# Fetching only the used rows in 19 of the last layer's 187 gathers

## The chip, the cores and the metric

The kernel runs on one core of a Trainium2 chip. The metric is the device time of one execution in microseconds. The profile's line numbers are those of the kernel's file before the change.

## The reference

Four graph layers run on one adjacency matrix of 2708 nodes with 128 features. Each layer's output is added to its input and the sum is normalised. The last layer, which the change touches, forms a message for every pair of nodes and sums the messages weighted by the adjacency:

```
s = node_feats @ msg_w[:, :D].T
d = node_feats @ msg_w[:, D:].T
messages = gelu(s[:, None, :] + d[None, :, :] + msg_b)
aggregated = einsum('ijd,ij->id', messages, adj)
h = gelu(concat([node_feats, aggregated]) @ upd_w.T + upd_b) + node_feats
out = (h - mean(h)) / sqrt(var(h) + 1e-5) * ln_w + ln_b
x = layernorm(x + out)
```

The adjacency is sparse (a node has a handful of neighbours), so only the messages of neighbours matter.

## The kernel before, in words

The first two layers multiply with the adjacency as a dense matrix on TensorE. While they run, VectorE finds each row's nonzero entries in descending order: `V` holds their values and `LIDX` their column numbers, for 22 blocks of 128 rows with up to `SLOTS` = 24 slots. Rows are sorted by their number of neighbours; `PERM` names the row that stands at each place, and `RANK` the place of each row. Block `b` needs no more than `CAPS[b]` slots, from 21 in the first block to 2 in the last, 187 in all. A row with fewer neighbours than its block's cap has the value zero in the remaining slots of `V`.

The third layer gathers one neighbour's row for every row (tile `ga`, line 918, 22 gathers), reads the rows in sorted order from DRAM into `OWN` (four loads by SyncE's queue), and forms the shares, the new features `X3` (line 1061) and the products `yd` for the last layer. `yd` is scattered to the DRAM table `TD` in the order of rows (line 1052, 22 scatters issued by GpSimd).

The last layer works by blocks in the order of `TURN`. For the block at position `k`:

- `gathers(k)` issues one indirect DMA on GpSimd (POOL) for each slot (line 1150): row `LIDX[p, b, s]` of `TD` goes to partition `p` of `G[:, s, :]`. The tile `G` comes from a pool of four buffers.
- `terms(k)` makes the row's own product on TensorE.
- `messages(k)` adds it to all gathered rows on VectorE (line 1179, tile `M`) and applies gelu on ScalarE (lines 1180 and 1181).
- `diagonals(k)` makes a diagonal matrix of each slot's values of `V` on ScalarE (line 1171, tile `W`), and `update(k)` multiplies the messages with them on TensorE, accumulating over the slots (line 1143). A zero in `V` so takes a slot's row out of the sum.
- `added` and `norms` finish the rows on VectorE, for sets of one to four blocks, and `stores` scatters them to the output (line 1250, GpSimd).

The loop is software-pipelined: in step `k` come the stores that are ready, the gathers of `k + 1`, its terms, then messages, diagonals and update.

`conditions()` checks, once, that the sparse path is valid: line 1102 marks the slots with a value above zero, line 1105 counts them for each block within its cap, and the count is compared with the row's degree. A violation raises the flag that has the general, dense path run afterwards. `X3B` (line 1097) is an addition of all normalised rows and a bias, which the norms use later.

The order on each engine is the order in which the program issues its instructions: `pinned` chains every instruction of an engine to the one before it. Waits between engines are put in by the tile framework, from the regions of tiles that instructions read and write. DMAs issued by GpSimd take eight semaphores in turn, so each waits for the one eight before it.

Of the kernel before, what the change touches and what calls it, by code (L numbers as in the profile page):

```python
# [24 lines left out]
F32 = mybir.dt.float32  # L25
# [6 lines left out]
ALU = mybir.AluOpType  # L32
AX = mybir.AxisListType
# [3 lines left out]
P = 128  # L37
# [9 lines left out]
SLOTS = 24  # L47
CAPS = (21, 13, 12, 11, 11, 10, 10, 9, 9, 9, 8, 8, 8, 7, 7, 6, 6, 6, 5, 5, 4, 2)


TABLE = (("kk", 32), ("lane", 128), ("part", 1), ("lt", 128), ("ident", 128))


def table():

    import numpy as np

    p = np.arange(P)[:, None]
    cols = {
        "kk": np.broadcast_to(np.arange(32), (P, 32)),  # L60
        "lane": np.broadcast_to(np.arange(P), (P, P)),
        "part": p,
        "lt": p < np.arange(P),
        "ident": p == np.arange(P),
    }
    return np.concatenate([cols[n].astype(np.float32) for n, _ in TABLE], axis=1)


@with_exitstack
def sparse_path(  # L70
# [27 lines left out]
    nc = tc.nc  # L98
    N, D = x.shape
    NB = -(-N // P)  # L100
# [10 lines left out]
    def rows(b):  # L111
        return min(P, N - b * P)
# [4 lines left out]
    const = ctx.enter_context(tc.tile_pool(name="s_const", bufs=1))  # L117
# [14 lines left out]
            X[:, k, :], x[k.start * P : k.stop * P, :].rearrange("(b p) d -> p b d", p=P)  # L132
        )
    nc.sync.dma_start(X[: rows(NF), NF, :], x[NF * P :, :])
    TAB = const.tile([P, sum(w for _, w in TABLE)], F32, name="TAB")
    nc.scalar.dma_start(TAB, consts)
    part, at = {}, 0
    for name, w in TABLE:
        part[name] = TAB[:, at : at + w]
        at += w  # L140
    ident = part["ident"]
# [21 lines left out]
    for h in range(HEADS):  # L163
        k = slice(h * HD, (h + 1) * HD)
# [34 lines left out]
    V = const.tile([P, NB, SLOTS], F32, name="V")  # L199
    nc.gpsimd.memset(V, 0.0)  # L200
    LIDX = const.tile([P, NB, SLOTS], U32, name="LIDX")
# [5 lines left out]
    V_, S_, T_, G_ = nc.vector, nc.scalar, nc.tensor, nc.gpsimd  # L207
    newest = {}

    def pinned(i):  # L210

        e = i.ins.engine
        if e in newest:
            tc.add_manual_dep(
                i.ins, newest[e].name,
                mybir.DependencyInfo(mybir.DependencyClass.NoSync, mybir.DependencyReason.DATA),
                reason="order",
            )
        newest[e] = i.ins
        return i  # L220
# [80 lines left out]
    f = lists.tile([P, NB], F32, name="f")  # L301
# [602 lines left out]
    TD = dram.tile([NP, D], F32, name="TD")  # L904
    late = ctx.enter_context(tc.tile_pool(name="late", bufs=1))
    OWN = late.tile([P, NB, W_], F32, name="OWN")
    X3 = late.tile([P, NB, D], F32, name="X3")
    with (
        tc.tile_pool(name="l2", bufs=1) as one,
        tc.tile_pool(name="l2b", bufs=2) as sb,  # L910
# [147 lines left out]
        def norm3(k):  # L1058
            zs, t = mid[k]
            for i, b in enumerate(sets[k]):  # L1060
                pinned(S_.activation(  # L1061
                    X3[:, b, :], XO[:, b, :], AF.Identity, bias=t[:, 0, i : i + 1],
                    scale=t[:, 3, i : i + 1],
# [21 lines left out]
    TURN = tuple(range(17)) + (19, 17, 20, 18, 21)  # L1085
    SETS = ((0, 4), (4, 8), (8, 12), (12, 16), (16, 19), (19, 21), (21, 22))
    with (
        tc.tile_pool(name="l3", bufs=1) as one,
        tc.tile_pool(name="l3_g", bufs=4) as gp,
        tc.tile_pool(name="l3_w", bufs=2) as wp,  # L1090
        tc.tile_pool(name="l3_o", bufs=3) as op,
        tc.tile_pool(name="l3_s", bufs=3) as sb,
# [3 lines left out]
        pinned(V_.tensor_tensor(W3[:, D : 2 * D], W3[:, :D], WD, ALU.add))  # L1096
        pinned(V_.tensor_tensor(X3B, X3, LN_B.unsqueeze(1).to_broadcast([P, NB, D]), ALU.add))

        def conditions():

            has = one.tile([P, NB, SLOTS], F32, name="has")
            pinned(V_.tensor_scalar(has, V, 0.0, None, ALU.is_gt))
            count = one.tile([P, NB], F32, name="count")
            for b in range(NB):
                pinned(V_.tensor_reduce(count[:, b : b + 1], has[:, b, : CAPS[b]], AX.X, ALU.add))
            pinned(V_.tensor_tensor(count, count, OWN[:, :, W_ - 1], ALU.not_equal))
            pinned(V_.tensor_reduce(FL[:, 4:5], count, AX.X, ALU.max))

            odd = one.tile([P, NB], F32, name="odd")
            pinned(V_.tensor_tensor(odd, CNT, HAVE, ALU.not_equal))  # L1110
            pinned(V_.tensor_reduce(FL[:, 2:3], odd, AX.X, ALU.max))
            same = one.tile([P, NB, SLOTS - 1], F32, name="same")
            pinned(V_.tensor_tensor(same, V[:, :, 1:], V[:, :, : SLOTS - 1], ALU.is_equal))
            pinned(V_.tensor_tensor(same, same, V[:, :, 1:], ALU.mult))
            pinned(V_.tensor_reduce(FL[:, 3:4], same, AX.XY, ALU.max))


            gap = one.tile([P, NB], F32, name="gap")
            pinned(V_.tensor_tensor(gap, V[:, :, 0], OWN[:, :, W_ - 2], ALU.max))
            pinned(V_.tensor_tensor(gap, gap, V[:, :, 1], ALU.subtract))  # L1120
            pinned(V_.tensor_scalar(gap, gap, 4e-7, None, ALU.is_lt))
            pinned(V_.scalar_tensor_tensor(gap, PERMF, float(N), gap, ALU.is_lt, ALU.mult))
            pinned(V_.tensor_reduce(FL[:, 5:6], gap, AX.X, ALU.max))
            lim = one.tile([P, 2], F32, name="lim")
            pinned(V_.tensor_reduce(lim[:, 0:1], OWN[:, :, 2 * D : W_ - 2], AX.XY, ALU.max))
            pinned(V_.tensor_reduce(lim[:, 1:2], OWN[:, :, 2 * D : W_ - 2], AX.XY, ALU.min))
            pinned(V_.tensor_scalar(lim[:, 1:2], lim[:, 1:2], -1.0, None, ALU.mult))
            pinned(V_.tensor_tensor(lim[:, 0:1], lim[:, 0:1], lim[:, 1:2], ALU.max))
            pinned(V_.tensor_scalar(FL[:, 7:8], lim[:, 0:1], 200.0, None, ALU.is_gt))
            worst = one.tile([P, 1], F32, name="worst")  # L1130
            pinned(V_.tensor_reduce(worst, FL, AX.X, ALU.max))
            t = ps.tile([P, P], F32, name="xT_ps")
            pinned(T_.transpose(t[:1, :], worst, ident))
            pinned(V_.tensor_reduce(worst[:1, :], t[:1, :], AX.X, ALU.max))
            pinned(V_.tensor_scalar(flag, worst[:1, :], 0.0, None, ALU.is_gt))

        place = {k: (i, k - lo) for i, (lo, hi) in enumerate(SETS) for k in range(lo, hi)}
        ys, sums, mids, Gs, Ms, Ws, ready = {}, {}, {}, {}, {}, {}, []
# [6 lines left out]
        def gathers(k):  # L1145
            b = TURN[k]
            n = CAPS[b]
            G = Gs[k] = gp.tile([P, CAPS[0], D], F32, name="G")
            for s in range(n):
                pinned(G_.indirect_dma_start(  # L1150
                    G[:, s, :], None, TD,
                    bass.IndirectOffsetOnAxis(ap=LIDX[:, b, s : s + 1], axis=0),
                ))

        def terms(k):

            t = ps.tile([P, P], F32, name="xT_ps")
            pinned(T_.transpose(t, X3[:, TURN[k], :], ident))
            xT = sb.tile([P, P], F32, name="xT")
# [14 lines left out]
        def messages(k):  # L1174
            n = CAPS[TURN[k]]
            G, m = Gs.pop(k), mids[k][0]
            M = Ms[k] = wp.tile([P, CAPS[0] + 1, D], F32, name="M")
            s_ = m[:, :D].unsqueeze(1).to_broadcast([P, n, D])
            pinned(V_.tensor_tensor(M[:, :n, :], G[:, :n, :], s_, ALU.add))  # L1179
            pinned(S_.activation(M[:, n, :], m[:, D : 2 * D], AF.Gelu))  # L1180
# [17 lines left out]
        def stats(dst, src):  # L1198
            st = small.tile([P, 6], F32, name="bn_s3")
            pinned(V_.bn_stats(st, src))  # L1200
            pinned(V_.bn_aggr(dst, st))

        def added(k):
            i, j = place[k]
            h = ys[i][:, j, :]
            pinned(V_.tensor_tensor(h, h, X3[:, TURN[k], :], ALU.add))
            stats(sums[i][:, j, :], h)
# [39 lines left out]
        def stores(k):  # L1247
            while ready and ready[0][0] <= k:
# [5 lines left out]
                tc.declare_no_dep(i.ins, group="OUT", reason="each row has a place of its own")  # L1254
                tc.add_to_no_dep_group("OUT", i.ins)

        gathers(0)
        conditions()
        terms(0)
        diagonals(0)  # L1260
        for k in range(NB):
            if k + 1 < NB:
                stores(k + 1)
                gathers(k + 1)
                terms(k + 1)
            messages(k)
            if k + 1 < NB:
                diagonals(k + 1)
            update(k)
            if k:  # L1270
                added(k - 1)
                i, j = place[k]
                if not j:
                    g = norms(i - 1)
                    for done in g:
                        if k == NB - 1 and done:
                            break
# [521 lines left out]
```

## Time and profile before

| what | us |
|---|---|
| median of 3 runs | 708.85 |
| lowest and highest of them | 706.58 and 709.79 |
| profiled execution | 709.3 |
| its span | 707.5 |
| POOL busy in the span | 378.5 |
| DVE busy | 393.0 |
| PE busy | 451.2 |
| ACT busy | 272.4 |

The span is what the profile covers of the execution; 1.8 us lie around it. A busy time is a sum over stages with different limits, so it doesn't say by itself what bounds the kernel; the chain of work that ended last and the groups of instructions, with what ended the idle time before each, are read for that.

### The profile page before, as it was taken

How to read it: one execution, taken by the hardware profiler on the slowest of the kernel's cores; microseconds unless marked ns; L12 is line 12 of the kernel's file. 1: busy time of each engine (PE TensorE's matmuls, PEld its weight loads, DVE VectorE, ACT ScalarE, POOL GpSimd, SP SyncE). 2: the span in 40 equal slices, each digit the busy share in tenths (PEclk: the TensorE clock that was granted, in tenths of full speed). 3: DMA queues.
4: the chain of work that ended last, by engine and by line, in shares of the span. 5: the costliest groups of instructions: out<-in, count | busy, mean ns of one | idle time of the engine just before them, and what ended most of it. 6: DMA issues, size and time to landing. Idle time of an engine off the chain costs nothing.

```text
span 707.5 us, 8193 instructions
## 1 busy us (share of the span) xinstructions
PE 451.2 (64%) x2565; PEld 301.7 (43%) x2565; DVE 393.0 (56%) x1138; ACT 272.4 (38%) x719; POOL 378.5 (53%) x449
## 2 busy tenths in 40 slices
PE   5889999996164999997511502066646546747461
PEld 5745445663152444464311501055536435545451
DVE  4767999999983856640208834111171251434466
ACT  3145655772330100174411574055335424444330
POOL 7002001221246776036577677777777777777761
PEclk9579999998556999999755555566776857788665
DMA  9968999996294999875254111222122122211210
GB/s 296 406 245 309 415 415 379 324 374 224 101 386 153 419 418 415 311 216 191 85 181 128 42 52 40 53 54 52 52 53 55 53 53 53 53 52 52 54 48 13
DMA packets 44400, 128.68 MB, mean 182 GB/s; under 512 B 7983, under 2 KB 19523, under 8 KB 38716
## 3 DMA queue, kind: packets, MB, share of 16 engines
q0 software_dynamic: 16832, 75.13, 30.2%
q1 hardware_dynamic: 21116, 49.66, 19.7%
q10 hardware_dynamic: 6400, 3.29, 1.7%
q8 instruction: 22, 0.36, 0.2%
q14 instruction: 30, 0.25, 0.1%
HBM read 119.29 MB, written 8.81 MB: 181 GB/s over the span
## 4 chain that ended last, share of the span: by engine, by line
DVE 27%; POOL 24%; PE 19%; issue 14%; DMA 9%; ACT 6%; SPq 0%; POOLq 0%; DVEq 0%; ACTq 0%
POOL G L1150 17%; PE acc L753 12%; DVE IX L580 9%; DVE cand L565 5%; DMA G<-TD,LIDX 4%; PE z L753 3%; POOL ga L918 2%; DMA TOP<-in_high 1%; POOL TS L693 1%; ACT squares L257 1%; PE w_ps L355 1%; ACT XD L267 1%; ACT X L1061 1%; DMA nat<-in_adjo,PERM 1%; POOL ln_r L262 1%
## 5 line engine op out<-in xcount | busy, mean ns | idle before, releaser
L1150 POOL DMA_INDIRECT G<-TD,LIDX x187 | 177.4, 948 | 58.7 <-issue 52.4
L1143 PE MATMUL aT_ps<-W,M 128*128 128x128 f32 x418 | 91.0, 394 | 112.5 <-ACT M L1180 105.1
L1143 PEld LDWEIGHTS aT_ps<-W,M 128*128 128x128 f32 x418 | 80.9, 292 | 126.4 <-ACT M L1180 114.0
L1179 DVE TENSOR_TENSOR M<-G,sd_ps 128x1152 f32<-128x1152 f32 (+11 forms) x22 | 28.3, 1287 | 159.0 <-DMA G<-TD,LIDX 142.8
L753 PE MATMUL acc<-ah,XD 128*128 128x512 f32 (+1 forms) x264 | 113.7, 568 | 1.0 <-ACT XD L626 1.0
L580 DVE FIND_INDEX8 IX<-V,nat 128x8 uint32<-128x2707 f32 x33 | 97.8, 2970 | 0.0
L830 ACT ACTIVATE sign<-ah 128x1536 bf16<-128x1536 f32 (+1 forms) x44 | 57.7, 1327 | 37.1 <-issue 26.8
L753 PE MATMUL acc<-ah,HS 128*128 128x512 f32 x132 | 63.3, 615 | 12.1 <-ACT HS L866 12.1
L753 PEld LDWEIGHTS acc<-ah,XD 128*128 128x128 f32 x264 | 47.9, 196 | 44.5 <-issue 41.4
L536 POOL DMA_INDIRECT nat<-in_adjo,PERM x22 | 21.5, 979 | 81.5 <-DVE IX L580 55.4
L1171 ACT ACTIVATE W<-TAB,V 128x128 f32<-128x128 f32 x187 | 56.8, 390 | 0.0
L558 DVE MAX8 V<-nat 128x8 f32<-128x2707 f32 x12 | 35.7, 2976 | 26.6 <-DMA nat<-in_adjo,PERM 26.6
L1180 ACT ACTIVATE M<-sd_ps 128x128 f32<-128x128 f32 x22 | 6.1, 278 | 113.2 <-DVE M L1179 113.2
L753 PEld LDWEIGHTS acc<-ah,HS 128*128 128x128 f32 x132 | 25.4, 196 | 44.7 <-issue 29.3
L866 ACT ACTIVATE HS<-HS,DS 128x128 f32<-128x128 f32 x22 | 8.4, 399 | 78.0 <-DMA HS<-TH,PERM 48.8
L565 DVE MAX8 cand<-nat 128x8 f32<-128x338 f32 (+3 forms) x88 | 34.3, 461 | 2.8 <-DMA nat<-in_adjo,PERM 2.8
L251 POOL TENSOR_SCALAR ln_a<-SUM 128x4 f32<-128x4 f32 (+1 forms) x12 | 2.9, 238 | 61.1 <-DVE XD L649 33.2
L1250 POOL DMA_INDIRECT out_x<-yo,PERM x22 | 22.1, 1003 | 18.5 <-DVE yo L1229 11.3
L861 POOL DMA_INDIRECT HS<-TH,PERM x22 | 21.0, 957 | 19.6 <-DMA TH<-H 10.1
L1052 POOL DMA_INDIRECT TD<-yd,PERM x22 | 24.2, 1102 | 9.6 <-ACT yd L1048 4.1
L753 PE MATMUL acc<-ah,H 128*128 128x512 f32 (+1 forms) x88 | 28.1, 462 | 0.0
L693 POOL DMA_INDIRECT TS<-XD,RANK x22 | 21.6, 982 | 11.3 <-issue 5.4
(281 smaller groups left out, 862.6 us busy)
## 6 DMA issues: line engine op xcount, KB each, us to landing
ah<-in_adjL SPq DMA_DIRECT2D x22, 768.0 KB, 13.5
ah<-in_adjR SPq DMA_DIRECT2D x44, 330.0 KB, 5.5
TOP<-in_high SPq DMA_DIRECT2D x5, 1354.0 KB, 13.0
ah<-in_adjL SPq DMA_DIRECT2D x22, 256.0 KB, 7.2
G<-TD,LIDX POOLq DMA_INDIRECT x187, 2.5
OWN<-TS SPq DMA_DIRECT2D x3, 798.0 KB, 8.5
TA<-XD ACTq DMA_DIRECT2D x5, 264.0 KB, 2.8
TH<-H ACTq DMA_DIRECT2D x5, 256.0 KB, 10.2
```

What stands on the lines that cost most here:

```text
L558: pinned(nc.vector.max(V[:, b, 0:8], t))
L565: pinned(nc.vector.max(c[:, 8 * k : 8 * k + 8], t[:, at]))
L580: pinned(nc.vector.max_index(IX[:, b, s], V[:, b, s], t))
L693: i = G_.indirect_dma_start(TS, bass.IndirectOffsetOnAxis(ap=RANK[:, b : b + 1], axis=0), XD[:, b, :], None,)
L753: pinned(T_.matmul(acc[i][:, :w], weights[:, n, :], a[:, i * BANK : i * BANK + w], start=n == 0, stop=n == NB - 1,))
L830: pinned(S_.activation(m[:, : hi - lo], a, AF.Sign))
L1052: i = G_.indirect_dma_start(TD, bass.IndirectOffsetOnAxis(ap=PERM[:, b : b + 1], axis=0), yd[:, i, :], None)
L1143: pinned(T_.matmul(t, a, b, start=n == 0, stop=n == len(parts) - 1))
L1150: pinned(G_.indirect_dma_start(G[:, s, :], None, TD, bass.IndirectOffsetOnAxis(ap=LIDX[:, b, s : s + 1], axis=0),))
L1171: pinned(S_.activation(W[:, s, :], ident, AF.Copy, scale=V[:, b, s : s + 1]))
L1179: pinned(V_.tensor_tensor(M[:, :n, :], G[:, :n, :], s_, ALU.add))
L1250: i = G_.indirect_dma_start(out, bass.IndirectOffsetOnAxis(ap=PERM[:, b : b + 1], axis=0), h, None, bounds_check=N - 1, oob_is_err=False,)
```

## The change

A table `LIMITS` names, for 19 pairs of block and slot, how many rows of the block are used; rows are sorted by their number of neighbours, so the used ones are the first. Each of those gathers then fetches only that many rows: 849 of 2432. The four buffers of `G` become four tiles named `spaces`, taken in turn, and the slots of the first three that are gathered in part at first use are set to zero before (line 1282 of the changed file), so that the rows not fetched hold finite numbers; later uses leave there what an earlier block had fetched. `V` is zero in these places.

The check counts only slots that the table calls used: `USES`, a 128 x 528 mask, comes with the table of constants, is loaded by SyncE's queue before the loads of `OWN`, and is multiplied into the marks. A row with more neighbours than the table allows thus raises the flag. The 22 counts become one over all 24 slots.

```diff
+LIMITS = {
+    0: {13: 122, 14: 65, 15: 41, 16: 23, 17: 14, 18: 10, 19: 9, 20: 8},
+    1: {12: 85}, 2: {11: 97}, 4: {10: 41}, 6: {9: 56}, 9: {8: 12}, 12: {7: 40}, 17: {5: 62},
+    19: {4: 48}, 20: {3: 68}, 21: {0: 26, 1: 22},
+}
+def used(b, s):
+    return LIMITS.get(b, {}).get(s, P) if s < CAPS[b] else 0
...
-    TAB = const.tile([P, sum(w for _, w in TABLE)], F32, name="TAB")
-    nc.scalar.dma_start(TAB, consts)
+    W_TAB = sum(w for n, w in TABLE if n != "uses")
+    TAB = const.tile([P, W_TAB], F32, name="TAB")
+    nc.scalar.dma_start(TAB, consts[:, :W_TAB])
...
     X3 = late.tile([P, NB, D], F32, name="X3")
+    USES = late.tile([P, NB, SLOTS], F32, name="USES")
+    nc.sync.dma_start(USES.rearrange("p b s -> p (b s)"), consts[:, W_TAB:])
...
-        tc.tile_pool(name="l3_g", bufs=4) as gp,
...
-            pinned(V_.tensor_scalar(has, V, 0.0, None, ALU.is_gt))
+            pinned(V_.scalar_tensor_tensor(has, V, 0.0, USES, ALU.is_gt, ALU.mult))
             count = one.tile([P, NB], F32, name="count")
-            for b in range(NB):
-                pinned(V_.tensor_reduce(count[:, b : b + 1], has[:, b, : CAPS[b]], AX.X, ALU.add))
+            pinned(V_.tensor_reduce(count, has, AX.X, ALU.add))
...
-            G = Gs[k] = gp.tile([P, CAPS[0], D], F32, name="G")
+            G = Gs[k] = spaces[k % 4]
             for s in range(n):
+                m = used(b, s)
                 pinned(G_.indirect_dma_start(
-                    G[:, s, :], None, TD,
-                    bass.IndirectOffsetOnAxis(ap=LIDX[:, b, s : s + 1], axis=0),
+                    G[:m, s, :], None, TD,
+                    bass.IndirectOffsetOnAxis(ap=LIDX[:m, b, s : s + 1], axis=0),
                 ))
...
+        spaces = [one.tile([P, CAPS[0], D], F32, name=f"G{k}") for k in range(4)]
+        for k in range(4):
+            n = CAPS[TURN[k]]
+            some = [s for s in range(n) if used(TURN[k], s) < P]
+            if some:
+                pinned(V_.memset(spaces[k][:, some[0] : n, :], 0.0))
         gathers(0)
```

More of the change, by code (lines that the diff above doesn't have):

```diff
@@ L48 @@
 CAPS = (21, 13, 12, 11, 11, 10, 10, 9, 9, 9, 8, 8, 8, 7, 7, 6, 6, 6, 5, 5, 4, 2)
-TABLE = (("kk", 32), ("lane", 128), ("part", 1), ("lt", 128), ("ident", 128))
+LIMITS = {
[3 rows of a table added]
+}
+def used(b, s):
+    return LIMITS.get(b, {}).get(s, P) if s < CAPS[b] else 0
+TABLE = (
+    ("kk", 32), ("lane", 128), ("part", 1), ("lt", 128), ("ident", 128),
+    ("uses", len(CAPS) * SLOTS),
+)
 def table():
@@ L64, in table @@
         "ident": p == np.arange(P),
+        "uses": p < np.array([[used(b, s) for s in range(SLOTS)] for b in range(len(CAPS))]).ravel(),
     }
@@ L134, in sparse_path @@
     nc.sync.dma_start(X[: rows(NF), NF, :], x[NF * P :, :])
-    TAB = const.tile([P, sum(w for _, w in TABLE)], F32, name="TAB")
-    nc.scalar.dma_start(TAB, consts)
+    W_TAB = sum(w for n, w in TABLE if n != "uses")
+    TAB = const.tile([P, W_TAB], F32, name="TAB")
+    nc.scalar.dma_start(TAB, consts[:, :W_TAB])
     part, at = {}, 0
-    for name, w in TABLE:
+    for name, w in TABLE[:-1]:
         part[name] = TAB[:, at : at + w]
```

## The prediction, made before the changed kernel ran

> **What bounds the kernel now.** I read the slices of the page first, then its chain and groups, then the timeline of POOL. From 429 to 684 us POOL is the engine that never rests, while PE, DVE and ACT stand near half. The chain and the costliest groups say why:
>
> ```profile
> POOL G L1150 17%; PE acc L753 12%; DVE IX L580 9%; DVE cand L565 5%; DMA G<-TD,LIDX 4%; PE z L753 3%; POOL ga L918 2%; DMA TOP<-in_high 1%; POOL TS L693 1%; ACT squares L257 1%; PE w_ps L355 1%; ACT XD L267 1%; ACT X L1061 1%; DMA nat<-in_adjo,PERM 1%; POOL ln_r L262 1%
> ...
> L1150 POOL DMA_INDIRECT G<-TD,LIDX x187 | 177.4, 948 | 58.7 <-issue 52.4
> ...
> L1179 DVE TENSOR_TENSOR M<-G,sd_ps 128x1152 f32<-128x1152 f32 (+11 forms) x22 | 28.3, 1287 | 159.0 <-DMA G<-TD,LIDX 142.8
> ```
>
> The gathers are the largest item of the chain. Each holds POOL for 948 ns, and the idle time before them is 52.4 us of "issue", 0.30 us each: nothing holds them back, and one leaves every 1.25 us. DVE waits 142.8 us for their data. A stretch in the middle of the stage agrees (us; then busy us of PE, PEld, DVE, ACT, POOL; clock; DMA share; GB/s):
>
> ```profile
> 480.00:520.00 40.00, 21.48 (x102) 17.95 (x100) 7.76 (x17) 15.09 (x45) 30.23 (x33) 0.76 0.21 52
> ```
>
> POOL with 30.2 busy us plus its issue gaps is full; the DMA engines are at 0.21. So bytes saved are worth nothing by themselves; what counts is the time that a partial gather holds POOL. All 187 gathers have 128 rows, so no row of the trace shows that. The nearest rows are the direct copies that POOL issues early on, of 128 rows (L171, L172, L174), 32 rows (L166) and one row cut into 16 pieces (L179):
>
> ```profile
> L166 POOL DMA_DIRECT2D AJI<-in_a x4 | 2.0, 508 | 1.0 <-DMA W<-in_w 1.0
> ...
> L179 POOL DMA_DIRECT2D BIAS<-in_msg_b x2 | 1.0, 505 | 0.4 <-issue 0.3
> ...
> L171 POOL DMA_DIRECT2D W<-in_msgT x1 | 0.6, 568 | 0.0
> ...
> L172 POOL DMA_DIRECT2D W<-in_updT x1 | 0.5, 539 | 0.0
> L174 POOL DMA_DIRECT2D UB<-in_updT x1 | 0.5, 534 | 0.0
> ```
>
> A direct copy costs about 0.54 us with 128 rows and 0.50 with 16 or 32 pieces. The gather's 0.944 (its median) is 0.40 more, for the work on indices; whether that 0.40 goes by rows is the question.
>
> **What the Trainium skill says.** (1) "Perfetto Trace Analysis", DMA Instruction — SWDGE (GPSIMD): the profile ends such an instruction when the last descriptor is written, not when data lands. The trace agrees: gathers last 0.94 us, the median landing is 2.5. (2) "DMA: Bandwidth & Descriptors", Anatomy of one DMA: generating descriptors is a small part, and "You can emit a lot of descriptors before the incremental cost shows up". The direct copies agree (0.04 us for 112 more); for gathers nothing shows it. (3) The same page, Why a DMA increments its semaphore by 16: a transfer runs on the largest k up to 16 that divides its row count; some direct copies are excepted. 97, 41 and 23 rows would go through one DMA engine, 122 and 62 through two. No run shows it yet. (4) "SBUF — State Buffer", Who interferes with whom: a DVE operation with two SBUF inputs blocks a GpSimd instruction that reads SBUF. The trace agrees:
>
> ```profile
> 370.03 0.95 DVE L967 TENSOR_TENSOR OWN<-OWN 128x768 f32<-128x768 f32 x1
> 370.46 1.34 POOL L918 DMA_INDIRECT ga<-TA,LIDX  x1 [0.30 <-issue]
> 372.10 0.94 POOL L918 DMA_INDIRECT ga<-TA,LIDX  x1 [0.30 <-issue]
> ...
> 422.83 3.09 DVE L1097 TENSOR_TENSOR X3B<-X,LN_B 128x2816 f32<-128x2816 f32 x1 [11.35 <-ACT X L1061]
> ...
> 423.52 3.23 POOL L1052 DMA_INDIRECT TD<-yd,PERM  x1 [0.30 <-DMA TD<-yd,PERM]
> 428.80 1.29 POOL L1150 DMA_INDIRECT G<-TD,LIDX  x1 [2.05 <-DVE odd L1110]
> ```
>
> Indirect transfers that start while such an operation runs end 0.82 us after it (370.98 and 371.80; 425.92 and 426.75).
>
> **The change, part by part.**
>
> *Which gathers count.* Near the end the chain leaves POOL: the last gather of position 18 (issued at 663.75) lands, DVE adds at 668.18, and from there PE, ACT and DVE carry the chain through the norms to 702. The gathers of positions 19 to 21 lie beside that. So the three partial ones among them (68, 26 and 22 rows) save nothing, and 16 count: 733 rows kept of 2048, 1315 saved.
>
> *POOL per row.* Index part 0.40 us/128 = 3.1 ns a row, descriptor part 0.04/112 = 0.4 ns: 3.5 ns, times 1315 = 4.6 us. Bounds: none of it by rows, 0; all of 0.944 by rows, 7.4 ns x 1315 = 9.7 us. Below nothing: see the first rival. I take 4.6: the index part is the one that a direct copy lacks, and its natural unit is the index.
>
> *Landing.* On the chain this matters only for position 18, whose last gather has 62 rows. A descriptor occupies its engine for about 0.21 x 1.25 us/8 = 33 ns (estimate, 128 rows over 16 engines). If two engines take 31 rows each, that is 23 more than 8, 0.8 us later; if all 16 take part, nothing. I take 0.4. Elsewhere a late landing is covered: POOL waits for the gather eight before, 8 x 1.25 = 10 us, and 97 rows on one engine take 3.2 us beyond the fixed part of 2.5. If descriptors took over 80 ns each, that cover would go and POOL would stall; up to 3 us for all, kept for the range. The four buffers leave three blocks of slack as before.
>
> *Start of the stage.* G's four spaces now lie in pool "l3", and the order of instructions shows that X3B has come to wait for all scatters of TD (SWDGE semaphores), where it waited for PE and ACT alone. The last scatter is then not blocked: 0.96 instead of 3.23 us, and the first gather starts 2.3 us earlier, at about 426.5. But X3B is released there too and blocks it until 426.5 + 3.09 + 0.82 = 430.4, where it now ends at 430.1. If the gather wins, the second one ends at that 430.4 instead of 431.35. So +0.3 or -0.9; the masking operation on V and USES has now two SBUF inputs, up to 0.4 more on one gather. I take 0, between -0.9 and +0.7.
>
> *DVE.* Three memsets (1024, 128 and 128 elements; those at L322 and L323 take 0.93 ns an element: 1.0 + 0.2 + 0.2 us), and one reduce of 528 elements (0.7 us) for 22 that took 1.6. DVE's next duty is the addition at 457.85 for which it idles 23.7 us: nothing, and under one microsecond if that cover were gone. Partial gather 13 waits for the memset, which is done ten gathers earlier.
>
> *SP.* The load of USES (264 KB, at the stage's some 400 GB/s 0.7 us) goes ahead of the four loads of OWN. Those wait for the last scatter of TS; USES waits for less, so it should be gone before. DVE idles between them for OWN, then for the gathers "ga" that POOL paces: nothing, at most 0.7 us if that cover fails.
>
> *Sum:* -4.6 + 0.4 + 0 = -4.2. The profiled execution took 709.3 us (span 707.5 and 1.8 around it), 0.45 above the median of 708.85: 705.1, or **704.7** by the median.
>
> **Rivals.**
>
> *Rounds per engine (slower).* If POOL writes descriptors in rounds of one per DMA engine, a full gather has 8 rounds and a partial one rows/k. By the skill's rule the 16 have 61, 5, 41, 23, 1, 1, 1, 1, 17, 97, 41, 4, 1, 4, 3 and 31: 332 instead of 128, 204 more. At the price of the direct copies, 0.04/7 = 6 ns a round, that is 1.2 us; if the index part goes by rounds too, 0.40/8 + 6 = 56 ns, 11.4 us. It decides from 3.5/204 = 17 ns a round on. Between the ends, at 30 ns: +6.1, and 0.8 for the landing: 715.7. For it: the cheap direct copies look as if sixteen descriptors were made at once. Against: that the rule holds for gathers isn't shown.
>
> *Fixed cost.* Index fetching costs 0.40 whatever the number, and POOL saves 0.4 ns x 1315 = 0.5 us: 708.8. For it: the page's sentence, and the bounds check of out_x (0.98 against 0.96) which adds only 0.02 us to 128 rows. The same result if the instruction were padded inside to 128 rows; that the 19 are issued with the named row counts stands in the order of instructions.
>
> *All by rows:* -9.7 + 0.4: 699.5.
>
> **Chances.** About 0.5% (3.5 us) is what a measurement of this kernel can tell from no change. Cost by rows, in part or whole, 0.50 (0.42 of it below 705.3); fixed 0.17 (0.12 within, 0.02 and 0.03 outside for the start of the stage and landings); rounds 0.33. Faster 0.44, same 0.20, slower 0.36. The likeliest case alone is 699 to 708; both signs hold most of the chance, so the range reaches from 699 (all by rows) to 716 (rounds at 30 ns), leaving out the dearest rounds.
>
> **What would show it.** Right: partial gathers shorter than 0.94 us in step with their rows (8 rows near 0.52, 122 near 0.92), X3B beginning at about 426.5, and the last out_x some 4 us earlier. Wrong: equal durations (fixed), or the gathers of 97, 41 and 122 rows above 0.94 while those of 8 to 14 lie below (rounds); a POOL wait for a DMA in the middle of the stage (landing). A DVE wait for OWN after 372 that grew would show USES in the way.

## The result and the profile after

The changed kernel takes **712.31 us** (median of 11 runs, 710.08 to 715.11) where the kernel before, run beside it, takes 708.13 (11 runs, 706.30 to 709.79). The ratio is 1.0060 with an interval of 1.0045 to 1.0074: it is slower, by some 4.2 us (3.2 to 5.2). The forecast was 704.7, faster. The time lies inside the range, on the other side of the kernel before.

The profiled execution took 710.08 us (span 708.3), the lowest of its runs, so the two profiles differ by less than the medians do. The page of the changed kernel, its chain and two groups (gathers are now L1169, the additions L1198):

```profile
POOL G L1169 17%; PE acc L770 12%; DVE IX L597 9%; DVE cand L582 5%; DMA G<-TD,LIDX 5%; PE z L770 3%; DMA TOP<-in_high 3%; POOL ga L938 2%; POOL TS L710 1%; ACT squares L274 1%; ACT XD L284 1%; DMA nat<-in_adjo,PERM 1%; POOL ln_r L279 1%; DVE XD L666 1%; DVE M L1198 1%
...
L1169 POOL DMA_INDIRECT G<-TD,LIDX x187 | 183.0, 978 | 58.7 <-issue 51.2
...
L1198 DVE TENSOR_TENSOR M<-G,sd_ps 128x1152 f32<-128x1152 f32 (+11 forms) x22 | 28.3, 1287 | 159.5 <-DMA G<-TD,LIDX 157.4
```

POOL's gathers still lead the chain, and almost nothing but their own issue holds them back (51.2 us, as before). But the 187 of them have grown from 177.4 to 183.0 us although nineteen of them fetch a third of their rows (849 of 2432), and the idle time of the additions in which DVE waits for them has grown from 142.8 to 157.4. Some 2.0 us of the growth is the first gather alone, which now stands beside `X3B` (1.29 us before, 3.27 after; the last scatter of `TD` went from 3.23 to 0.95). A mean of 978 ns hides the rest. POOL's timeline (start, duration) at the first position, from slot 12 to slot 20, shows it; the rows fetched are 128, then 122, 65, 41, 23, 14, 10, 9 and 8:

```profile
442.43 0.94 POOL L1169 DMA_INDIRECT G<-TD,LIDX  x1 [0.30 <-issue]
443.68 1.69 POOL L1169 DMA_INDIRECT G<-TD,LIDX  x1 [0.31 <-issue]
445.67 0.93 POOL L1169 DMA_INDIRECT G<-TD,LIDX  x1 [0.30 <-issue]
446.90 1.41 POOL L1169 DMA_INDIRECT G<-TD,LIDX  x1 [0.30 <-issue]
448.61 1.15 POOL L1169 DMA_INDIRECT G<-TD,LIDX  x1 [0.30 <-issue]
450.07 0.87 POOL L1169 DMA_INDIRECT G<-TD,LIDX  x1 [0.30 <-issue]
451.24 0.87 POOL L1169 DMA_INDIRECT G<-TD,LIDX  x1 [0.30 <-issue]
452.42 0.85 POOL L1169 DMA_INDIRECT G<-TD,LIDX  x1 [0.30 <-issue]
453.58 0.88 POOL L1169 DMA_INDIRECT G<-TD,LIDX  x1 [0.30 <-issue]
...
484.95 2.15 POOL L1169 DMA_INDIRECT G<-TD,LIDX  x1 [0.30 <-issue]
```

The last line is the gather of 97 rows. A gather of 122 rows takes nearly twice as long as one of 128, one of 97 more than twice, one of 23 more than one of 65. Even 8 rows save only 0.06 us. Take k as in the prediction's third point, the largest divisor of the row count up to 16, and call rows/k the rounds. The durations with k below 16 then lie close to one line, drawn through these same points: **0.87 us + 13.3 ns x (rounds - 1)**.

| rows | k | rounds | line, us | measured, us |
|---|---|---|---|---|
| 8 to 14 (five counts) | 8 to 14 | 1 | 0.87 | 0.85 to 0.89 |
| 22, 26 | 11, 13 | 2 | 0.88 | 1.02, 0.91 |
| 40, 56 | 10, 14 | 4 | 0.91 | 0.91, 0.92 |
| 65 | 13 | 5 | 0.92 | 0.93 |
| 68, 85 | 4, 5 | 17 | 1.08 | 1.11, 1.09 |
| 23 | 1 | 23 | 1.16 | 1.15 |
| 62 | 2 | 31 | 1.27 | 1.27 |
| 41 | 1 | 41 | 1.40 | 1.41 |
| 122 | 2 | 61 | 1.67 | 1.69 |
| 97 | 1 | 97 | 2.15 | 2.15 |

The 22 rows are the one outlier; three other executions have 0.92 for them. The 48 rows, with k = 16, take 0.88. The 16 partial gathers that count, summed from the timeline, take 18.17 us where 16 full ones take 16 x 0.944 = 15.10: +3.1.

That the rows really go to k shares can be seen in the packets that POOL's DMAs moved (packets, MB, share of the 16 engines' span), first before, then after:

```profile
q0 software_dynamic: 16832, 75.13, 30.2%
```

```profile
q0 software_dynamic: 17440, 74.34, 29.3%
```

There are fewer bytes, but 608 packets more. Their sizes, read from the packet records of the trace, tell why (a row has 512 B). A full gather leaves 16 packets of 4096 B, eight rows each. The gather of 65 rows leaves 13 of 2560 B, five rows each. That of 97 rows leaves one share with all the rows (12 packets of 4096 B and one of 512), and 15 shares without a row in which 4 bytes move for each of the 97 rounds (388 B: 12 packets of 32 B and one of 4). Every round so has a part for each of sixteen shares, however few of them carry rows.

### The profile page after: what moved, and what is told of

Its sections match the earlier page's. It is cut to its first block, busy times and chain, and to the rows that moved or that the text cites. A ratio compares the mean times of both kernels' runs of the same rounds, so it can differ in the third digit from the quotient of the medians.

```text
span 708.3 us, 8184 instructions
## 1 busy us (share of the span) xinstructions
PE 447.3 (63%) x2565; PEld 298.9 (42%) x2565; DVE 392.8 (55%) x1120; ACT 272.7 (39%) x719; POOL 382.8 (54%) x449
## 4 chain that ended last, share of the span: by engine, by line
DVE 26%; POOL 24%; PE 18%; issue 14%; DMA 12%; ACT 4%; SPq 1%; POOLq 0%; DVEq 0%; ACTq 0%
POOL G L1169 17%; PE acc L770 12%; DVE IX L597 9%; DVE cand L582 5%; DMA G<-TD,LIDX 5%; PE z L770 3%; DMA TOP<-in_high 3%; POOL ga L938 2%; POOL TS L710 1%; ACT squares L274 1%; ACT XD L284 1%; DMA nat<-in_adjo,PERM 1%; POOL ln_r L279 1%; DVE XD L666 1%; DVE M L1198 1%
## 5 line engine op out<-in xcount | busy, mean ns | idle before, releaser
L1169 POOL DMA_INDIRECT G<-TD,LIDX x187 | 183.0, 978 | 58.7 <-issue 51.2
L1198 DVE TENSOR_TENSOR M<-G,sd_ps 128x1152 f32<-128x1152 f32 (+11 forms) x22 | 28.3, 1287 | 159.5 <-DMA G<-TD,LIDX 157.4
L938 POOL DMA_INDIRECT ga<-TA,LIDX x22 | 23.6, 1075 | 6.7 <-issue 6.7
```

The lines of the kernel that those rows point to most:

```text
L938: pinned(G_.indirect_dma_start(ga[:, i, :], None, TA, bass.IndirectOffsetOnAxis(ap=LIDX[:, b, 0:1], axis=0)))
L1169: pinned(G_.indirect_dma_start(G[:m, s, :], None, TD, bass.IndirectOffsetOnAxis(ap=LIDX[:m, b, s : s + 1], axis=0),))
```

## The experiments

Two theories stood after the result. **Rounds**: the price of a gather goes by its rounds on the fullest DMA engine, so row counts that 16 divides cost nothing extra. **Side work**: the four tiles in place of the pool, the memsets, USES and the merged count delay the stage, and the long gathers only add to it. Each ratio below is to the kernel before, run beside it on the same chip.

### Full rows, all else as changed

```diff
-                m = used(b, s)
+                m = P
```

> The changed kernel with all 187 gathers fetching 128 rows again; the four tiles, the memsets, the mask USES with its load and the new count stay. Theory 'rounds' (a gather holds POOL for 0.87 us and 13.3 ns for each further round, rounds being rows over the largest divisor of the row count up to 16): every gather back at 0.94 us, the 3.3 us that the 16 partial gathers cost gone, time within 1.5 us of the kernel before (ratio 0.998 to 1.002). Rival 'side work' (the memsets, the mask, the load or X3B's new wait are what costs): still some 4 us slower than before, ratio about 1.006.

Measured: 707.82 us against 708.14, ratio 0.9994 (0.9979 to 1.0009); all nineteen gathers back at 0.94 to 0.98 us. The side work costs nothing that can be measured, and the row counts carry the loss.

### Row counts rounded up to multiples of 16

```diff
-                m = used(b, s)
+                m = -(-used(b, s) // 16) * 16
```

> The changed kernel with each partial row count rounded up to a multiple of 16 (8, 9, 10, 12 and 14 to 16; 22, 23 and 26 to 32; 40, 41 and 48 to 48; 56 and 62 to 64; 65 and 68 to 80; 85 to 96; 97 to 112; 122 to 128). Rounds: one to eight rounds each, POOL durations 0.87 (16 rows) to 0.94 us (128), all below or at a full gather's; 77 rounds fewer than full gathers, 1.0 us, so 4 us faster than the changed kernel and about 1 us faster than before, ratio to before 0.997 to 1.000. Rival 'rows' (a short gather is dear for having few rows, for instance by a general path taken below 128): the 48-row gathers stay well above 0.94 us and the time some us above before. Side work: 1.005.

Measured: 706.89 us, ratio 0.9981 (0.9966 to 0.9996). The timeline of POOL in this kernel, the same eight gathers, now of 128, 80, 48, 32 and four times 16 rows:

```profile
444.10 0.94 POOL L1169 DMA_INDIRECT G<-TD,LIDX  x1 [0.30 <-issue]
445.34 0.92 POOL L1169 DMA_INDIRECT G<-TD,LIDX  x1 [0.30 <-issue]
446.56 0.87 POOL L1169 DMA_INDIRECT G<-TD,LIDX  x1 [0.30 <-issue]
447.74 0.86 POOL L1169 DMA_INDIRECT G<-TD,LIDX  x1 [0.30 <-issue]
448.91 0.85 POOL L1169 DMA_INDIRECT G<-TD,LIDX  x1 [0.30 <-issue]
450.06 0.83 POOL L1169 DMA_INDIRECT G<-TD,LIDX  x1 [0.30 <-issue]
451.19 0.84 POOL L1169 DMA_INDIRECT G<-TD,LIDX  x1 [0.30 <-issue]
452.34 0.83 POOL L1169 DMA_INDIRECT G<-TD,LIDX  x1 [0.30 <-issue]
```

More rows fetched, less time: 48 rows take 0.87 where 41 took 1.41. The whole saving of a gather cut from 128 rows to 16 is 0.94 - 0.84 = 0.10 us, over seven rounds some 14 ns each, near the other kernel's 13.3: a round costs about the same whether sixteen shares carry rows or one. The 16 gathers that count now sum to 14.1 us, 1.0 under full ones, and the kernel gains about that (1.3 by the ratio, 0.3 to 2.4).

### 113 rows against 112

Two sizes one row apart, in the 18 gathers that use at most 112 rows:

```diff
-                m = used(b, s)
+                m = 113 if used(b, s) <= 112 else P
```

> The changed kernel with 113 rows in each of the 18 gathers that use 112 or fewer (the one with 122 fetches 128). 113 has no divisor up to 16 but 1. Rounds: each holds POOL for 0.87 + 112 x 0.0133 = 2.36 us; 15 of them lie before the point where the chain leaves POOL, 15 x 1.42 = 21 us on POOL, and some 2 to 3 us for the later landing of the last of these: 20 to 25 us slower than before. Rows: 113 rows cost as 112 do, within 1 us of the run with 112.

and the same with 112 in place of 113:

> As the run with 113 rows, with one row fewer: 112, which 16 divides. Rounds: 7 rounds, 0.93 to 0.95 us each, time within 1.5 us of before. Rows: as with 113. Side work: both about 4 us slower than before.

The groups of POOL, of the kernel with 113 rows; then three gathers of its timeline, 113 rows each; then the same slots in the kernel with 112:

```profile
L1169 POOL DMA_INDIRECT G<-TD,LIDX x187 | 205.3, 1098 | 58.7 <-issue 51.5 <-DMA G<-TD,LIDX 2.4 <-DMA TD<-yd,PERM 2.1
```

```profile
447.20 2.38 POOL L1169 DMA_INDIRECT G<-TD,LIDX  x1 [0.30 <-issue]
449.88 2.36 POOL L1169 DMA_INDIRECT G<-TD,LIDX  x1 [0.30 <-issue]
452.54 2.35 POOL L1169 DMA_INDIRECT G<-TD,LIDX  x1 [0.30 <-issue]
```

```profile
444.10 0.94 POOL L1169 DMA_INDIRECT G<-TD,LIDX  x1 [0.31 <-issue]
445.34 0.93 POOL L1169 DMA_INDIRECT G<-TD,LIDX  x1 [0.30 <-issue]
446.58 0.92 POOL L1169 DMA_INDIRECT G<-TD,LIDX  x1 [0.30 <-issue]
```

113 rows: 733.7 us, ratio 1.0343 (1.0318 to 1.0369). 112 rows: 707.84 us, 0.9994 (0.9979 to 1.0009). One row more in 18 gathers costs some 25 us (24.7 by the two ratios, 25.9 by the medians, of four runs with 113 rows). The line found above gives 0.87 + 112 x 13.3 ns = 2.36 for a prime count, and that is what is measured. Fifteen of the 18 lie at positions up to 18, which is 15 x 1.43 = 21.4 us of POOL; the landing of position 18's last gather adds 1.7 (4.66 us from its end on POOL to the addition, against 2.97 with 112 rows), and the tail after the last store 1.1 (more of it below): 24.2 together.

### On another chip: without USES, and X3B in pieces

Three kernels ran on one other chip: the changed one without USES (the 22 counts restored), and two in which X3B, one addition of 3.09 us, is made in 22 pieces after the checks of the lists, in the kernel before and in the one with rounded counts:

```diff
-            pinned(V_.scalar_tensor_tensor(has, V, 0.0, USES, ALU.is_gt, ALU.mult))
+            pinned(V_.tensor_scalar(has, V, 0.0, None, ALU.is_gt))
```

```diff
-        pinned(V_.tensor_tensor(X3B, X3, LN_B.unsqueeze(1).to_broadcast([P, NB, D]), ALU.add))
...
         conditions()
+        for b in range(NB):
+            pinned(V_.tensor_tensor(X3B[:, b, :], X3[:, b, :], LN_B, ALU.add))
```

> The changed kernel, partial gathers as there, but with the check of the kernel before: no mask USES, no load of it ahead of OWN, 22 counts instead of one. Rounds: as slow as the changed kernel, 1.004 to 1.008 of before, gathers of 97 and 41 rows still at 2.15 and 1.41 us. Side work (the load or the mask costs part of it): 1 us or more faster than the changed kernel.

> The kernel before with X3B made in 22 additions of one block each (0.28 us) after the conditions, where VectorE waits for the first gathers, instead of one addition of 3.09 us ahead of them. Lock theory (a GpSimd indirect DMA that starts while a VectorE operation reads two SBUF inputs ends 0.82 us after it): the last scatter of TD takes 0.96 us instead of 3.23, the first gather starts 2.3 us earlier and no gather exceeds some 1.2 us; 2 to 2.5 us faster than before, ratio 0.9965. Rival (start of the stage is covered elsewhere, or the 22 pieces block the gathers they meet): within 0.7 us of before, with 22 gathers lengthened.

> The changed kernel with row counts rounded up to multiples of 16 and X3B in 22 pieces after the conditions. If both effects stand and add: 1.0 to 1.3 us from the rounds and 2 to 2.5 us from the first gather, which is no longer blocked by X3B: some 3.3 us faster than before, ratio 0.994 to 0.997. If the memsets or the mask block the first gathers in X3B's place: 0.998, as with the rounding alone.

On that chip the kernel before itself took 794.4 us, and the ratios are 1.0000, 0.9999 and 0.9998, each within 0.002 of 1. ACT's groups show another bound. Before the 22 copies of the last layer ACT waits 154 to 161 us in all for a release that the profile calls "remote", one that it can't put down to any instruction or DMA. Here is the line of the second of the three, the kernel before with X3B in pieces:

```profile
L1189 ACT COPY aT<-aT_ps 128x128 f32<-128x128 f32 x22 | 5.8, 265 | 170.5 <-remote 156.7 <-PE aT_ps L1142 7.6 <-issue 4.7
```

With the last layer held there, gathers of any length lie beside the wait, and the comparison says nothing on the theories. The granted clock of TensorE was lower there, too (0.73 to 0.74, against 0.76 to 0.78 on the other chips). What that wait is was not found. The durations on POOL are still to be read: without USES the partial gathers last as with it (1.69, 0.93, 1.41, 1.15 and 2.16 for 122, 65, 41, 23 and 97 rows). And the pieces were no help: back to back they run for 4.5 us, and one gather is blocked nearly as long. POOL in the kernel with rounded counts, its eighth gather:

```profile
437.75 0.94 POOL L1168 DMA_INDIRECT G<-TD,LIDX  x1 [0.30 <-issue]
439.00 4.49 POOL L1168 DMA_INDIRECT G<-TD,LIDX  x1 [0.30 <-DMA G<-TD,LIDX]
```

### X3B in spread pieces, and both kernels again

A gather that meets DVE's additions is blocked for as long as they run without a break. So two pieces were put ahead of each of the first eleven messages, where DVE waits for gathers anyway; once on the kernel before, once with rounded counts. On the same chip ran the changed kernel without USES and the changed kernel as it is.

```diff
         def messages(k):
...
+            for i in range(2 * k, min(2 * k + 2, NB)):
+                b = TURN[i]
+                pinned(V_.tensor_tensor(X3B[:, b, :], X3[:, b, :], LN_B, ALU.add))
```

> The kernel before with X3B made in 22 additions of one block, two ahead of each of the first eleven additions of messages, where VectorE waits for gathers. After e6, in which the 22 pieces back to back blocked one indirect DMA for 3.7 us: pieces that stand alone block at most the end of one gather each, by under 0.2 us as they last 0.28 us. Lock theory: the last scatter of TD takes 0.96 us instead of 3.23, no gather over 1.4 us; 2 to 2.5 us faster than before, ratio 0.9965. Rival (the start of the stage is covered elsewhere): within 0.7 us of before.

> The changed kernel with row counts rounded up to multiples of 16 and X3B spread as in e8. If both effects stand and add: 1.0 to 1.3 us from the rounds and 2.3 us from the first gather (0.96 to 1.3 us long instead of 3.27): some 3.5 us faster than before, ratio 0.995. If the memsets and the mask block the first gathers in X3B's place: about 0.998, as with the rounding alone.

> The kernel of e5 once more, on a chip on which the gathers bound the last layer: the changed kernel, partial gathers as there, with the check of the kernel before (no mask USES, no load of it, 22 counts). Rounds: as slow as the changed kernel within 1 us, 1.004 to 1.008 of before. Side work: 1 us or more faster than the changed kernel.

> The changed kernel again, beside the others of this call: 1.0045 to 1.0075 of before, gathers of 97, 41 and 122 rows at 2.15, 1.41 and 1.69 us. The gap between the last scatter of TD and the first full gather after it shows whether the start of the stage gives or takes: no more than 0.5 us by the first trace.

| kernel | us | ratio to before (708.29) | interval |
|---|---|---|---|
| before, X3B spread | 706.83 | 0.9980 | 0.9968 to 0.9992 |
| rounded counts, X3B spread | **705.21** | 0.9955 | 0.9940 to 0.9970 |
| changed, without USES | 713.35 | 1.0074 | 1.0055 to 1.0092 |
| changed, as it is | 712.02 | 1.0049 | 1.0032 to 1.0067 |

USES and the merged count are no part of the loss. The spread pieces take the block off the first gather, as POOL's timeline of the kernel in the second row shows, the last scatter and the first two gathers:

```profile
422.69 0.96 POOL L1072 DMA_INDIRECT TD<-yd,PERM  x1 [0.31 <-DMA TD<-yd,PERM]
425.70 0.97 POOL L1168 DMA_INDIRECT G<-TD,LIDX  x1 [2.05 <-DMA TD<-yd,PERM]
426.98 0.97 POOL L1168 DMA_INDIRECT G<-TD,LIDX  x1 [0.30 <-issue]
```

From the last scatter's start to the second gather it is 4.3 us here and 6.9 in the kernel before. Of these 2.6 us the kernel before with spread pieces shows 1.5 in its time (0.6 to 2.3), fewer than the 2 to 2.5 expected. The profiles have more: from the last scatter's start to the end of the span it is 280.8 us in place of 284.0, and in the execution with spread pieces that scatter started 0.8 us later. So the rest was not lost in the last layer; the medians leave it open. Rounded counts and spread pieces together give 3.1 us under the kernel before, the best version of the study.

### One gather of 97 rows alone

The tail of the changed kernel was longer, too. From the start of the last out_x store to the end of the span it is 5.1 us before (702.44 to 707.5) and 6.3 after (701.97 to 708.3). SP's waits in the last 11 us (waited for: us in total, times, longest), first of the kernel before, then of the changed one:

```profile
SPq L1790 <- PEq L1790: 1.6, 2, 1.0
```

```profile
SPq L1816 <- PEq L1816: 2.8, 2, 2.3
```

In the five profiles whose gathers have counts with k below 16 this wait is 2.6 to 2.8 us and the tail 6.1 to 6.4; in the eight others 1.2 to 1.6 and 4.7 to 5.4.

The view names PE's queue because that came last; the records of instructions in the traces show what all the engines wait for. After the last store POOL carries out a closing instruction, DRAIN, and 0.17 us after its end SP, ACT, DVE and PE go on within 0.02 us of each other. It lasts 3.31 us in the kernel before and 4.56 in the changed one, which is the whole difference of the tails. It is 4.55 to 4.56 in all four profiles of the changed gathers, 4.40 with 113 rows, and 2.93 to 3.55 in the eight others. The last run asks whether one such gather brings it:

```diff
-                m = -(-used(b, s) // 16) * 16
+                m = 97 if used(b, s) == 97 else -(-used(b, s) // 16) * 16
```

> All partial gathers are rounded up to multiples of 16 rows as in the kernel with ceil16, except the one of 97 rows, which fetches 97. Both theories expect that gather at 2.15 us for 0.93, and so about 1.2 us more than with all of them rounded (some 708.1 where the kernel before has 708.3). They differ on the program's end. So far the span ended 6.1 to 6.4 us after the start of the last out_x store in the five profiles whose gathers have row counts with a largest divisor below 16 (the changed kernel twice, without USES twice, 113 rows), and 4.7 to 5.4 us after it in the eight others; the difference is SP's wait for PE's queue at the program's last line (2.6 to 2.8 us against 1.2 to 1.6). Theory A, one such gather is enough and the end costs a fixed 1.3 us: 6.1 to 6.4 here, and about 709.4 in all. Rival B, the end goes by the number of such gathers: 1 of 19 adds under 0.1 us, 4.7 to 5.0 here, and 708.1 in all.

Measured: 708.72 us, ratio 1.0002 (0.9982 to 1.0021), some 1.5 us above the kernel with all counts rounded by the two ratios; the gather takes 2.15 us. The tail is 705.2 - 699.94 = 5.3, and POOL's DRAIN 3.49 us: not the fixed 1.3 us of theory A, and more than B's share of one gather in 19. With all counts rounded the DRAIN took 2.93 and 2.96 us on two chips (3.19 on the one where the last layer was held), so in single profiles one such gather adds some 0.3 to 0.6 of the 1.6 us that the changed kernel has over the rounded one. It doesn't go by the rounds either, as 18 gathers of 113 rows have less than the changed kernel. What POOL does in it stays open.

## Why the prediction was wrong, point by point

*What bounds the kernel* was right: POOL's gathers carry the chain up to position 18, and time put on POOL appears in the end.

***POOL per row*, -4.6: the step that failed.** This term took the gather's 0.40 us over a direct copy for a price by rows, 3.1 ns each, with 0.4 ns for the descriptor. The runs show no price by rows. From 128 rows to 16 a gather loses 0.10 us, 0.9 ns a row where all counts are multiples of 16, and 0.84 us stays whatever is left out. The index part is therefore mostly fixed. And a count that 16 doesn't divide pays 13.3 ns for each round on the fewer engines. In place of -4.6 stands +3.1 by the durations; POOL's position against the last scatter, just past position 18's last gather, moved by +3.3 us between the two profiles (241.2 to 244.4 after that scatter's start).

*The rival of rounds* had the mechanism right, with its 332 rounds, and was given 0.33. Its price was between 6 and 56 ns, and 30 was taken; measured 13.3. That lies below the 17 ns from which it was to decide. By the line, the 332 rounds less the first of each of the 16 gathers are 316 x 13.3 ns = 4.2 us, and the start at 0.87 for 0.944 gives back 16 x 0.07 = 1.2: 3.0, where 3.1 were measured. That the difference passes 3.5 us is due to the tail (below). What could have turned the forecast stood in the prediction itself: the rule of the Trainium skill ("DMA: Bandwidth & Descriptors", Why a DMA increments its semaphore by 16) gives the number of engines for each count, and the packets of the 97 rows in one share confirm it here for gathers, as do 112 against 113 rows, 0.93 against 2.36 us. "That the rule holds for gathers isn't shown" was given too much weight: the page excepts some direct copies, and no gathers. The page's sentence on many descriptors (Anatomy of one DMA) held for 16 to 128 rows in multiples of 16 (0.10 us), and not for 113.

*Landing*, +0.4: wrong in sign. The 62-row gather of position 18 ends later on POOL, but the addition starts 2.36 us after that end (2.35 and 2.75 in two other executions of the changed gathers), against 3.49 in the kernel before (3.1 on average over seven kernels with a multiple of 16 there, from 2.69 up): some 0.6 us given back. The data don't move earlier, while POOL still writes: the first packet of this gather starts 0.62 us after POOL's end, and 0.70 with 64 rows there. Why the addition starts sooner all the same stays open. No stall for a gather eight back appeared in the changed kernel.

*Start of the stage*, 0: right. The second gather starts 6.6 us after the last scatter's start (6.9 before), gather 13 21.8 after it, 21.9 before. X3B did come to stand behind the scatters and did block the first gather instead of the last scatter, with an end 0.85 us after its own, as in the prediction's fourth point (0.82 there). DVE's and POOL's lines at the start of the changed stage:

```profile
424.24 3.09 DVE L1116 TENSOR_TENSOR X3B<-X,LN_B 128x2816 f32<-128x2816 f32 x1 [14.37 <-DMA TD<-yd,PERM]
```

```profile
424.91 3.27 POOL L1169 DMA_INDIRECT G<-TD,LIDX  x1 [2.06 <-DMA TD<-yd,PERM]
428.49 0.96 POOL L1169 DMA_INDIRECT G<-TD,LIDX  x1 [0.30 <-issue]
429.75 0.95 POOL L1169 DMA_INDIRECT G<-TD,LIDX  x1 [0.30 <-issue]
431.00 1.14 POOL L1169 DMA_INDIRECT G<-TD,LIDX  x1 [0.30 <-issue]
```

*DVE* and *SP*, 0: right. Full rows with all the side work 0.9994; without USES no gain.

*The sum* against the medians' +4.2: POOL +3.3, landing -0.6, the tail after the last store +1.25 (6.33 less 5.06), together some +3.9. The tail was not in the prediction at all; it was put at nothing. Three profiles of the changed gathers (one without USES) have 286.4, 287.8 and 287.9 us from the last scatter's start to the end of the span; the kernel before and the one with full rows have 284.0 and 283.9, so +3.4. The +0.8 between the two profiled spans is less, in part because in that execution of the changed kernel the last scatter started 1.6 us earlier; in the eleven profiles on the chips where the gathers bound the last layer it starts anywhere from 421.1 to 424.6 us.

## What to carry to other kernels

Before the row count of a gather is cut, divide it: with the largest divisor up to 16 as k, rows/k is what it pays for, 13.3 ns a round here, on top of some 0.85 us. Round the count up to a multiple of 16; the extra rows cost nothing here, where bytes don't bound. And fewer rows per gather save little when the instruction is nearly all fixed cost (0.84 of 0.94 us). By these figures a gather left out would save more than nine shortened from 128 rows to 16 (an estimate; no run left one out).

## What the runs showed of the hardware that was not expected

- One row decides: 113 rows hold POOL for 2.36 us, 112 for 0.93. The shares of a gather that carry no rows still move 4 bytes in each round (15 of 388 B each beside the 97 rows).
- 22 short additions on DVE with two SBUF inputs, issued back to back, block a gather as a single long one does (4.49 us for one gather while the pieces ran); spread apart they don't.
- The program's end, after the last store, was some 1.25 us longer with many gathers of k below 16: POOL's closing DRAIN took 4.56 us in place of 3.31.
- On one chip the same kernel took 794 us with waits named "remote" before ACT's copies of the last layer (154 to 161 us in all), and 3 us more of POOL then changed nothing.
